# Start of a convolution and attention kernel: zero matmuls during the first load, first loads in two parts, `norms` two chunks later, the last v copied by two engines, the exp table set in the v phase

## The chip, the cores and the metric

The kernel runs on one core of a Trainium2 chip. It was written in Bass with the Tile framework. A core has a matmul engine (TensorE, PE in the profile), three engines for elementwise work (VectorE = DVE, ScalarE = ACT, GpSimd = POOL), SyncE (SP), which here only issues DMAs, a working memory (SBUF) and the matmul's result memory (PSUM, eight banks of 128 x 512 f32). ACT, SP and POOL each issue DMAs from a queue of their own, in program order, and an instruction behind a DMA in the program of ACT can only begin when that DMA could be issued.

The metric is the time of one execution on the device in microseconds. The profile is of one more execution, which took a little longer; all durations below are from it.

## The reference

Two layers on an input x of (2, 256, 64, 64). The first computes an attention over all 4096 positions with 8 heads of 32 channels, a 1x1 convolution of x and the result together, and a blend by an upsampled mask. The second has a channel gate, an attention in windows of 8 x 8, and two grouped 7 x 7 convolutions. The part that the change touches is the projection at the head of the first layer:

```python
def proj(Wp, bp):
    p = _conv1x1(x, Wp, bp)
    return p.reshape(B * NUM_HEADS, hd, num).transpose(0, 2, 1)
q = proj(Wq, bq) / math.sqrt(hd)
k = proj(Wk, bk)
v = proj(Wv, bv)
attn = jax.nn.softmax(jnp.einsum('bnd,bmd->bnm', q, k), axis=-1)
fuse = jnp.einsum('bnm,bmd->bnd', attn, v)
```

## The kernel before

Everything is f32. The order of the instructions on each engine is that of the program text (`tc.manual_schedule()`), and waits are derived from who writes and reads which tile. The work has four stages.

**q and k (lines 382 to 465, 0 to about 124 us).** x is cut into 16 chunks (2 images, 8 chunks of 512 positions, `chunks`). For each chunk PE computes q and k: for each, four matmuls of 128x128 weights by 128x512 (`L438`, output halves g by input halves kc), into a pair of PSUM banks from a pool of three such pairs. ACT copies the pair out with the bias (`qst`, `kst`, `L448`), squares it (`sq`, `L451`), and DVE takes maxima of the squares over groups of 16 (`top16`, `L457`). SP stores q and k to DRAM (`q_s`, `k_s`) and loads the x of a later chunk (`load_chunk`, `L406`), four chunks ahead. ACT's own queue also loads the weights: `WqT`, `WkT`, `WvT`, `bq`, `bk` before the loop (`L385`, `L394`), and four more small or large ones after each of the first chunks (`pending`, `L464`), from `WfT` to `ca_w2`. `prepared` is a generator that interleaves other preparation (masks, batch norms, convolution weights) with the chunks; it has a Sqrt on ACT near chunk 5 (`L285`).

Every DMA of the ACT and SP queues signals on one of eight semaphores, dealt out in turn; a DMA waits until the one that held its semaphore before has landed.

**norms (lines 411 to 418).** After every four chunks PE sums the `top16` maxima of those four over the channels of a head (four small matmuls, x8 in the profile) and DVE takes their maximum. In the text of before they come behind q and k of chunks 4, 8 and 12, and, for the last four chunks, behind v of chunk 0. The end of it is a flag (`L496` to `L501`, behind v of chunk 1) which says whether the exps need a shift; all engines read it at `L1299` and branch. In the run measured here no shift is needed.

**v (lines 470 to 516, about 124 to 180 us).** For each chunk eight matmuls with x as weights (`L475`), one ACT copy of 128x1024 out of the PSUM pair (`vst`, `L483`), two stores by POOL. Behind v of chunk 2 there is a small product for the bias (`bvf`, `L508`).

**Attention and the rest (from 180 us).** `psum.close()` gives PSUM to another layout; the first scores reuse banks that the v copies free. There are 1024 slots: scores of one key block for four heads (`sa`, `L643`, sixteen matmul records), exp on ACT (`ea`, `L656`, three instructions), the product with v (`ava`, `L695`), and a running sum of the exps on DVE (`L701`). Scores run two slots ahead of products. The sums of the first 64 slots are folded by POOL's DMAs into `folda` and summed over heads by PE (`dna`, `L729`). ACT's table of functions is set to exp by a one-element activation just ahead of the loop (`warm`, `L1235`). Between the slots PE also gets the matmuls of the second layer, and the convolutions end the kernel.

```python
if i and i % 4 == 0:
    norms(i // 4 - 1, last)
last = tops
```

Of the kernel before, what the change touches and what calls it, by code (L numbers as in the profile page):

```python
# [10 lines left out]
F32 = mybir.dt.float32  # L11
I32 = mybir.dt.int32
AF = mybir.ActivationFunctionType
# [6 lines left out]
P = 128  # L20
KC = C // P
CH = 512
# [12 lines left out]
WS = 8  # L35
NW = W // WS
# [21 lines left out]
def conv_seq_kernel(ctx: ExitStack, tc: tile.TileContext, a, out):  # L58
    nc = tc.nc
# [13 lines left out]
    def psum2(name):  # L73
        return ps["pair"].tile([P, 2, CH], F32, tag="s", name=name)

    def psum1(name):
        return ps["one"].tile([P, CH], F32, tag="h", name=name)
# [6 lines left out]
    ones = const.tile([P, P], F32, name="ones")  # L84
# [15 lines left out]
    for h in range(HEADS0):  # L100
        n, rows = (0, 32) if h < HG else (1 + (h - HG) // 2, 64)
        p = rows * (h % HG if h < HG else h % 2)
# [270 lines left out]
    warm = const.tile([1, 1], F32, name="warm")  # L373
    with (
        tc.tile_pool(name="mk", bufs=2) as mk,
        tc.tile_pool(name="w0", bufs=1) as w0,
        tc.tile_pool(name="st0", bufs=2) as st0,
        tc.tile_pool(name="x0", bufs=1) as x0,
        tc.tile_pool(name="cw", bufs=1) as cwp,
        tc.manual_schedule(),  # L380
    ):
        wqk = []
        for n in ("WqT", "WkT", "WvT"):
            t = w0.tile([P, KC, C], F32, name=n)
            nc.scalar.dma_start(t, a[n].rearrange("(k p) o -> p k o", p=P))  # L385
            wqk.append(t)
        wq, wk, wv = wqk
        bias = {}
        for n in ("bq", "bk"):

            t = w0.tile([P, KC], F32, name=n)
            src = a[n].rearrange("h d (g k) -> k (h d) g", g=KC)
            for k in range(2):
                nc.scalar.dma_start(t[64 * k : 64 * k + 64, :], src[k])  # L394
            bias[n] = t

        chunks = [(b, c) for b in range(B) for c in range(NCHUNK)]
        xs0 = []

        def load_chunk():  # L400
            if len(xs0) == len(chunks):
                return
            b, c = chunks[len(xs0)]
            x = x0.tile([P, KC, CH], F32, name=f"x0_{b}_{c}")
            src = a["x"][b].rearrange("(k p) h w -> p k (h w)", p=P)
            nc.sync.dma_start(x, src[:, :, c * CH : (c + 1) * CH])  # L406
            xs0.append(x)

        def norms(i, tops):
            s = psum1(f"nrm_{i}")
            for n in range(2 * KC):
                s_ = s[32 * n : 32 * n + 32, 0 : CH // 4]
                nc.tensor.matmul(
                    s_, headsum, tops[:, n].rearrange("p c n -> p (c n)"), start=True, stop=True
                )
            nc.vector.tensor_reduce(nm[:, i : i + 1], s[:, 0 : CH // 4], AX.X, ALU.max)

        prepared = prepare(mk, cwp)  # L420
        next(prepared)
        for _ in range(3):
            load_chunk()
        last = None
        for i, (b, c) in enumerate(chunks):
            load_chunk()
            x = xs0[i]
            sq = st0.tile([P, 2 * KC, CH], F32, tag="sq", name=f"sq_{b}_{c}")
            if i % 4 == 0:
                tops = st0.tile([P, 2 * KC, 4, CH // 16], F32, tag="top16", name=f"top16_{i}")  # L430
            for n, w in (("q", wq), ("k", wk)):
                s = psum2(f"{n}0_{b}_{c}")
                for g in range(KC):
                    for kc in range(KC):
                        rhs = x[:, kc, :]
                        if n == "q":
                            rhs = rhs.rearrange("p (r w c) -> p w r c", r=WS, w=NW)
                        nc.tensor.matmul(  # L438
                            s[:, g, :],
                            w[:, kc, g * P : (g + 1) * P],  # L440
                            rhs,
                            start=(kc == 0),
                            stop=(kc == KC - 1),
                        )
                t = st0.tile([P, KC, CH], F32, tag=n, name=f"{n}st_{b}_{c}")
                bt = bias["b" + n]
                for g in range(KC):
                    nc.scalar.activation(  # L448
                        t[:, g, :], s[:, g, :], AF.Identity, bias=bt[:, g : g + 1]
                    )  # L450
                nc.scalar.activation(sq[:, 0:KC] if n == "q" else sq[:, KC:], t, AF.Square)  # L451
                if n == "q":
                    nc.sync.dma_start(q_s[b, c], t.rearrange("p g n -> p (g n)"))
                else:
                    for g in range(KC):
                        nc.sync.dma_start(k_s[b, g, c], t[:, g, :])
            nc.vector.tensor_reduce(  # L457
                tops[:, :, i % 4], sq.rearrange("p g (n f) -> p g n f", f=16), AX.X, ALU.max
            )
            if i and i % 4 == 0:  # L460
                norms(i // 4 - 1, last)
            last = tops
            for t, src in pending[4 * i : 4 * i + 4]:
                nc.scalar.dma_start(t, src)  # L464
            next(prepared, None)


        row = psum1("toprow")
        top = w0.tile([P, 1], F32, name="top")
        for i, (b, c) in enumerate(chunks):  # L470
            s = psum2(f"v0_{b}_{c}")
            sv = s.rearrange("p a (t o) -> p (a t) o", t=2)
            for m in range(4):
                for kc in range(KC):
                    nc.tensor.matmul(  # L475
                        sv[:, m, :],
                        xs0[i][:, kc, m * P : (m + 1) * P],
                        wv[:, kc, :],
                        start=(kc == 0),
                        stop=(kc == KC - 1),  # L480
                    )
            v = st0.tile([P, KC, 4, P], F32, tag="v", name=f"vst_{b}_{c}")
            nc.scalar.copy(  # L483
                v.rearrange("p g m d -> p m g d"),
                sv.rearrange("p m (g d) -> p m g d", g=KC),
            )
            for g in range(KC):
                nc.gpsimd.dma_start(v_s[b, g, c], v[:, g].rearrange("p m d -> p (m d)"))
            if i == 0:
                norms(len(chunks) // 4 - 1, last)  # L490
                nc.vector.tensor_reduce(top, nm, AX.X, ALU.max)
            elif i == 1:

                nc.tensor.matmul(row[0:1, 0:P], top, ident, start=True, stop=True)
                qk2 = w0.tile([1, 2], F32, name="qk2")
                nc.vector.tensor_reduce(  # L496
                    qk2, row[0:1, 0:P].rearrange("p (i r) -> p i r", i=2), AX.X, ALU.max
                )
                prod = w0.tile([1, 1], F32, name="prod")
                nc.vector.tensor_mul(prod, qk2[:, 0:1], qk2[:, 1:2])  # L500
                nc.vector.tensor_scalar(flag, prod, (SAFE / SCALE0) ** 2, None, ALU.is_le)  # L501
            elif i == 2:


                s = psum1("bvf")
                for oc in range(KC):
                    for kc in range(KC):
                        nc.tensor.matmul(  # L508
                            s[:, oc : oc + 1],
                            wf[:, KC + kc, oc * P : (oc + 1) * P],  # L510
                            bv[:, kc : kc + 1],
                            start=(kc == 0),
                            stop=(kc == KC - 1),
                        )
                nc.vector.tensor_add(bf, s[:, 0:KC], bf)
            next(prepared, None)
        for _ in prepared:
            pass

    psum.close()  # L520

# [11 lines left out]
    def pipeline(arm, shifted, pools):  # L533
# [40 lines left out]
        def load_q(b, c):  # L574
            q = qp.tile([P, KC, CH], F32, tag="q", name=f"q{arm}_{b}_{c}")
            nc.sync.dma_start(q, q_s[b, c].rearrange("p (g n) -> p g n", g=KC))
            qts[b, c] = q
# [654 lines left out]

        banded = bands()

        nc.scalar.activation(warm, ones[0:1, 0:1], AF.Exp)  # L1235
        load_q(0, 0)
        for n in range(AHEAD):
            load_piece(n)
# [130 lines left out]
```

## Time and profile before

| what | us |
|---|---|
| three runs, median | 2900.6 (2898.96 to 2902.66) |
| the profiled execution | 2911.19, span 2909.3 |
| PE busy in the span | 2863.8 |
| first matmul | 5.47 |
| end of the last v matmul, about | 179.6 |
| first exp of the attention | 182.11 |

How to read it: the span is the time from the first to the last instruction of the profiled execution, and the execution's own time is 1.9 us more. Times in the chain of waits and in the timelines count from the span's start. A matmul of f32 shows as two records, so the eight records of q in a chunk are four instructions. `x8` behind an operation is the number of records that were merged, and their common length stands ahead. In brackets the idle time of the engine ahead of the group, with what ended it. `ACTq` and `SPq` are the queues' own work, the issuing of DMAs.

### The profile page before, as it was taken

To read this page: it belongs to the slowest core of one execution; us is meant where nothing else is said; L and a number is where in the kernel's file an instruction comes from. 1 tells how busy PE (TensorE), PEld (TensorE's weight loads), DVE (VectorE), ACT (ScalarE), POOL (GpSimd) and SP (SyncE) were. 2 spreads that over 40 slices of the span, in tenths; PEclk is the share of its full clock that TensorE was granted. 3 is DMA by queue.
4 is the path that set the end of the run, shared out by engine and by line. 5 is a ranking of instruction groups with operands and counts; after the bars stand their busy time and mean duration, and the time that the engine had idled before them with its cause. 6 is when DMAs were issued, how large, how long until landed. Compare 5 with 4: busy or idle time off the path is not lost.

```text
span 2909.3 us, 85471 instructions
## 1 busy us (share of the span) xinstructions
PE 2863.8 (98%) x37002; PEld 827.4 (28%) x37002; DVE 2435.4 (84%) x1344; ACT 2455.3 (84%) x4145; POOL 569.1 (20%) x937
## 2 busy tenths in 40 slices
PE   8999999999999999999999999999999999999998
PEld 3551122222222222222222222222222222222675
DVE  4249999899999999998999999999999899999211
ACT  5569989898989898989989898989899898989433
POOL 8111111111111212121111011111212110000476
PEclk9999999999999999999999999999999999999999
DMA  8545433433253434353333324343435342232565
GB/s 253 209 163 189 146 89 76 94 82 89 65 101 79 105 77 105 79 95 86 82 92 79 88 68 98 78 97 78 100 82 97 82 88 78 67 113 88 137 197 134
DMA packets 245690, 305.65 MB, mean 105 GB/s; under 512 B 121208, under 2 KB 137772, under 8 KB 245048
## 3 DMA queue, kind: packets, MB, share of 16 engines
q1 hardware_dynamic: 200068, 231.51, 28.6%
q0 software_dynamic: 40464, 65.79, 12.2%
q8 instruction: 293, 4.80, 0.7%
q10 hardware_dynamic: 4772, 2.79, 0.3%
q14 instruction: 93, 0.76, 0.1%
HBM read 221.88 MB, written 66.39 MB: 99 GB/s over the span
## 4 chain that ended last, share of the span: by engine, by line
PE 89%; DMA 4%; POOL 2%; issue 2%; DVE 2%; ACT 1%; ACTq 0%; POOLq 0%; DVEq 0%
PE sa L643 34%; PE ava L695 33%; PE qka L529 4%; PE hya L529 3%; PE c1a L1093 2%; PE vwa L529 2%; PE opa L529 2%; PE c2a L1118 2%; PE v L475 2%; PE q L438 2%; PE k L438 1%; DMA xs<-xo 1%; POOL out_dram L1172 1%; DMA invs<-inva 1%; DMA folda<-suma 1%
## 5 line engine op out<-in xcount | busy, mean ns | idle before, releaser
L656 ACT ACTIVATE ea<-sa 128x512 f32<-128x512 f32 (+1 forms) x3072 | 2037.0, 746 | 51.5 <-PE sa L643 24.5
L643 PE MATMUL sa<-qa,ka 32*64 32x512 f32 x16384 | 1147.5, 613 | 1.5 <-ACT vst L483 1.2
L701 DVE TENSOR_TENSOR suma<-suma,ea 128x2048 f32<-128x2048 f32 x480 | 1096.4, 2284 | 5.7 <-ACT ea L656 0.5
L695 PE MATMUL ava<-ea,va 128*32 128x512 f32 x8192 | 1091.8, 605 | 1.0
L701 DVE TENSOR_TENSOR odda<-odda,ea 128x2048 f32<-128x2048 f32 x420 | 958.4, 2282 | 45.9 <-ACT ea L656 45.8
L673 POOL DMA_DIRECT2D folda<-suma x336 | 235.7, 903 | 1669.6 <-DVE suma L703 981.6
L643 PEld LDWEIGHTS sa<-qa,ka 32*64 32x64 f32 x16384 | 242.4, 129 | 786.2 <-ACT ea L656 716.3
L695 PEld LDWEIGHTS ava<-ea,va 128*32 128x32 f32 x8192 | 161.6, 108 | 834.9 <-issue 805.4
L1172 POOL DMA_DIRECT2D out_dram<-za x212 | 119.7, 573 | 58.7 <-DVE za L1145 31.8
L701 DVE TENSOR_TENSOR suma<-ea,ea 128x2048 f32<-128x2048 f32 x32 | 73.2, 2286 | 58.9 <-ACT ea L656 58.9
L529 PE MATMUL qka<-ua,qkv_w 128*32 128x512 f32 x1024 | 115.8, 592 | 0.1
L785 ACT ACTIVATE ta<-hya,bf 128x512 f32<-128x512 f32 x32 | 20.3, 684 | 100.6 <-PE hya L529 94.6
L1024 POOL DMA_DIRECT2D xs<-xo x94 | 72.3, 1058 | 139.6 <-DVE xo L1009 137.4
L457 DVE TENSOR_REDUCE top<-sq 128x128 f32<-128x2048 f32 x16 | 36.6, 2285 | 74.8 <-ACT sq L451 74.8
L741 POOL DMA_DIRECT2D invs<-inva x62 | 34.2, 560 | 296.9 <-DVE inva L756 296.0
L1118 PE MATMUL c2a<-yca,wa 32*64 32x192 f32 (+1 forms) x2912 | 84.4, 367 | 3.7 <-issue 3.4
L903 ACT ACTIVATE ewa<-ewa,mxwa 128x64 f32<-128x64 f32 x256 | 85.3, 346 | 1.5 <-DVE mxwa L894 1.5
L1129 ACT ACTIVATE za<-c2a 128x384 f32<-128x384 f32 x64 | 27.8, 487 | 66.0 <-PE c2a L1118 38.5
L789 DVE TENSOR_TENSOR ta<-ta,mca 128x512 f32<-128x512 f32 x32 | 22.0, 688 | 67.1 <-ACT ta L785 67.1
L861 ACT ACTIVATE qka<-qka,qkv_b 128x512 f32<-128x512 f32 x64 | 40.2, 680 | 39.5 <-PE qka L529 39.5
L1118 PEld LDWEIGHTS c2a<-yca,wa 32*64 32x64 f32 x2912 | 67.5, 191 | 21.1 <-issue 13.9
L1145 DVE TENSOR_TENSOR za<-za,xla 128x768 f32<-128x768 f32 x16 | 15.3, 959 | 65.2 <-DMA out_dram<-za 36.4
(143 smaller groups left out, 1721.3 us busy)
## 6 DMA issues: line engine op xcount, KB each, us to landing
ka<-ks SPq DMA_DIRECT2D x256, 256.0 KB
va<-vs SPq DMA_DIRECT2D x256, 256.0 KB
wa<-ws SPq DMA_DIRECT2D x17, 896.0 KB
ws<-zeros SPq DMA_DIRECT2D x16, 896.0 KB
folda<-suma POOLq DMA_DIRECT2D x224, 64.0 KB, 3.2
folda<-suma POOLq DMA_DIRECT2D x112, 128.0 KB, 3.8
xs<-xo POOLq DMA_DIRECT2D x78, 140.0 KB, 8.1
x<-in_x_dram SPq DMA_DIRECT2D x16, 512.0 KB
```

Source lines behind the costliest of these rows:

```text
L438: nc.tensor.matmul(s[:, g, :], w[:, kc, g * P : (g + 1) * P], rhs, start=(kc == 0), stop=(kc == KC - 1),)
L475: nc.tensor.matmul(sv[:, m, :], xs0[i][:, kc, m * P : (m + 1) * P], wv[:, kc, :], start=(kc == 0), stop=(kc == KC - 1),)
L529: nc.tensor.matmul(out[o : o + 32], weights[:, o : o + 32], x, start=start, stop=stop)
L643: nc.tensor.matmul(heads[j][o], k[r, cols][:, o], q[r, g, :], start=True, stop=not shifted)
L656: nc.scalar.activation(e[:, h, :], tile, AF.Exp, scale=SCALE0)
L673: nc.gpsimd.dma_start(dst[p : p + rows], total[rows * k : rows * k + rows, h, :], accum_op=ALU.add if k else ALU.bypass,)
L695: nc.tensor.matmul(av[r, :], v[:, m % PB, r], e[:, j, :], start=start, stop=stop)
L701: nc.vector.tensor_add(total, first.pop(m % chains, total), e)
L903: nc.scalar.activation(e[:, n, :], e[:, n, :], AF.Exp, bias=mx[:, n : n + 1], accum_out=rs[:, n : n + 1],)
L1024: eng.dma_start(x_s[b, n, p + r0 : p + r1].rearrange("r g w -> g r w"), xo[64 * h : 64 * h + 64, oc, r0 - WS * c : r1 - WS * c, :],)
L1118: nc.tensor.matmul(tiles[j // 2][o, j % 2, 0 : n * W], w[r, d, o], y[r, 0:n, d : d + W], start=(d == 0), stop=(d == KS - 1),)
L1172: eng.dma_start(*args)
```

## The change

It has five parts, all in the first two stages.

- Two matmuls of zeros, 128x128 by 128x512, stand first on PE. DVE sets the zeros.
- `WqT` and x of chunk 0 are loaded by two DMAs each, one for each input half kc, instead of one. For chunk 0 the four matmuls of q, and of k, run with kc outside and the output half g inside.
- `norms` of chunks 0 to 3 stands behind q and k of chunk 6 instead of 4, the next ones behind 10 and 14, and the last behind v of chunk 1 instead of 0. `last` keeps the maxima of the last complete four. The flag is computed behind v of chunk 4 instead of 1, `bvf` behind 6 instead of 2.
- The last v is copied in halves, one by ACT and one by DVE.
- The one-element exp stands behind v of chunk 12 (with what is left of `prepared`, which had come to its end during the q and k stage), and no longer ahead of the attention.

```diff
+        idle = w0.tile([P, CH], F32, name="idle")
+        nc.vector.memset(idle, 0.0)
+        s = psum1("idle")
+        for n in range(2):
+            nc.tensor.matmul(s, idle[:, 0:P], idle, start=(n == 0), stop=(n == 1))
         wqk = []
         for n in ("WqT", "WkT", "WvT"):
             t = w0.tile([P, KC, C], F32, name=n)
-            nc.scalar.dma_start(t, a[n].rearrange("(k p) o -> p k o", p=P))
+            src = a[n].rearrange("(k p) o -> p k o", p=P)
+            for kc in range(KC if n == "WqT" else 1):
+                ks = slice(kc, kc + 1) if n == "WqT" else slice(0, KC)
+                nc.scalar.dma_start(t[:, ks], src[:, ks])
...
-            nc.sync.dma_start(x, src[:, :, c * CH : (c + 1) * CH])
+            for kc in range(1 if xs0 else KC):
+                ks = slice(0, KC) if xs0 else slice(kc, kc + 1)
+                nc.sync.dma_start(x[:, ks], src[:, ks, c * CH : (c + 1) * CH])
...
-                for g in range(KC):
-                    for kc in range(KC):
...
+                order = [(g, kc) for g in range(KC) for kc in range(KC)]
+                if i == 0:
+                    order.sort(key=lambda gk: gk[1])
+                for g, kc in order:
...
-            if i and i % 4 == 0:
+            if i > 4 and i % 4 == 2:
                 norms(i // 4 - 1, last)
-            last = tops
+            if i % 4 == 3:
+                last = tops
...
-            nc.scalar.copy(
-                v.rearrange("p g m d -> p m g d"),
-                sv.rearrange("p m (g d) -> p m g d", g=KC),
-            )
+            evict = [(nc.scalar.copy, slice(0, 4))]
+            if i == len(chunks) - 1:
+                evict = [(nc.scalar.copy, slice(0, 2)), (nc.vector.tensor_copy, slice(2, 4))]
+            for copy, ms in evict:
+                copy(
+                    v[:, :, ms].rearrange("p g m d -> p m g d"),
+                    sv[:, ms].rearrange("p m (g d) -> p m g d", g=KC),
+                )
...
-            if i == 0:
+            if i == 1:
                 norms(len(chunks) // 4 - 1, last)
...
-            elif i == 1:
+            elif i == 4:
...
-            elif i == 2:
+            elif i == 6:
...
-        for _ in prepared:
-            pass
+            if i == len(chunks) - 4:
+                for _ in prepared:
+                    pass
+                nc.scalar.activation(warm, ones[0:1, 0:1], AF.Exp)
...
-        nc.scalar.activation(warm, ones[0:1, 0:1], AF.Exp)
         load_q(0, 0)
```

More of the change, by code (lines that the diff above doesn't have):

```diff
@@ L432, in conv_seq_kernel @@
                 s = psum2(f"{n}0_{b}_{c}")
-                for g in range(KC):
-                    for kc in range(KC):
[L435 to L443, printed above, removed]
-                        )
+                order = [(g, kc) for g in range(KC) for kc in range(KC)]
+                if i == 0:
+                    order.sort(key=lambda gk: gk[1])
+                for g, kc in order:
+                    rhs = x[:, kc, :]
+                    if n == "q":
+                        rhs = rhs.rearrange("p (r w c) -> p w r c", r=WS, w=NW)
+                    nc.tensor.matmul(
+                        s[:, g, :],
+                        w[:, kc, g * P : (g + 1) * P],
+                        rhs,
+                        start=(kc == 0),
+                        stop=(kc == KC - 1),
+                    )
                 t = st0.tile([P, KC, CH], F32, tag=n, name=f"{n}st_{b}_{c}")
@@ L482, in conv_seq_kernel @@
             v = st0.tile([P, KC, 4, P], F32, tag="v", name=f"vst_{b}_{c}")
-            nc.scalar.copy(
-                v.rearrange("p g m d -> p m g d"),
-                sv.rearrange("p m (g d) -> p m g d", g=KC),
-            )
+            evict = [(nc.scalar.copy, slice(0, 4))]
[5 more added lines that the diff above has]
+                    sv[:, ms].rearrange("p m (g d) -> p m g d", g=KC),
+                )
             for g in range(KC):
                 nc.gpsimd.dma_start(v_s[b, g, c], v[:, g].rearrange("p m d -> p (m d)"))
-            if i == 0:
+            if i == 1:
                 norms(len(chunks) // 4 - 1, last)
                 nc.vector.tensor_reduce(top, nm, AX.X, ALU.max)
-            elif i == 1:
+            elif i == 4:
                 nc.tensor.matmul(row[0:1, 0:P], top, ident, start=True, stop=True)
```

## The prediction

> **What bounds the kernel now.** I read the page's busy shares first, then a table of busy time by stage, and then only the two ends of the stage that the change edits: the chain of waits, and the timelines of ScalarE (ACT) and TensorE (PE).
>
> ```profile
> PE 2863.8 (98%) x37002; PEld 827.4 (28%) x37002; DVE 2435.4 (84%) x1344; ACT 2455.3 (84%) x4145; POOL 569.1 (20%) x937
> ...
> 0.00:43.65 43.65, 36.38 (x80) 15.79 (x81) 10.44 (x14) 21.95 (x29) 33.54 (x83) 1.00 0.88 247
> ...
> 340.00:2700.00 2360.00, 2354.41 (x30040) 568.01 (x30032) 2191.65 (x1148) 2127.52 (x3627) 345.33 (x524) 1.00 0.38 87
> ```
>
> The table's rows give the stretch, its length, then the busy time of PE, PE's weight loads, DVE, ACT and POOL, the clock and the DMA share. From 340 to 2700 us PE is busy 2354.4 of 2360 us. So what the start saves is kept: the loop behind it has one bound, PE, and is shifted as a whole. At the start PE is busy 36.4 of 43.65 us: all that the change can win lies in holes of 7.3 us there (and in slow passes, below), 1.4 us before 125.77, and 1.5 us from 179.6 to 188.
>
> ```profile
> 18.23 10.72 DMA qkv_b<-in_qkv_b_dram
> ...
> 28.97 7.03 DMA out_w<-in_out_w_dram
> ...
> 41.22 2.30 DVE top L457
> 43.52 0.14 issue
> 43.65 0.43 PE nrm L415 x8
> ```
>
> The chain says that PE is not what sets the end of the first 43 us. PE runs q and k of chunk 0 (5.47 to 14.40), and then the chain leaves it: ACT stands in its own queue behind weight DMAs (10.72 us until `qkv_b` had landed, 7.03 us until `out_w` had), its squares come late, DVE's maximum comes later still, and PE stops 1.80 us for it in `norms`. ACT was out of that queue when `qst` of chunk 3 began, at 36.59. From the timelines:
>
> ```profile
> 10.40 1.28 ACT L448 ACT_TABLE_LOAD   x1 [10.40 <-DMA bk<-in_bk_dram]
> ...
> 125.77 0.42 PE L415 MATMUL nrm<-top,headsum 128*32 128x128 f32 x8 [1.40 <-DVE top L457]
> ...
> 180.71 1.28 ACT L1235 ACT_TABLE_LOAD   x1
> ...
> 180.79 3.02 PE L643 MATMUL sa<-qa,ka 32*64 32x512 f32 x32 [1.19 <-ACT vst L483]
> ...
> 182.11 18.44 ACT L656 ACTIVATE ea<-sa 128x512 f32<-128x512 f32 x28
> ```
>
> Each line has start, length, engine, line and operation, and in brackets the idle time before and what ended it. The first is where ACT begins; the second is the next hole (1.40 us, the fourth `norms`); the others are the third: PE waits 1.19 us for the last v copy (179.68, 1.01 us), and the exps start at 182.11, behind the table load.
>
> **What the Trainium skill says.** "TensorE: Matmul & The Clock Gate", Part 1: the array starts at half clock and is let go after a busy window of about 3.4 us, which runs free of the kernel. The trace agrees: weight loads of q start at 6.49, 7.34, 8.20 and 9.05 and then at 9.50 and 9.93, so a pass took 0.85 us until 3.6 us after the first matmul, and 0.43 from there. "ScalarE: Activation LUTs", What ACT_TABLE_LOAD costs: 1.28 us plus a drain of 1.38; the trace has the 1.28, and no drain (copy over at 180.69, load at 180.71). Table sets, same page: copies sit in every set, so the three v copies behind an early exp set cause no new load; before, the v copies followed Sqrt without one. "DMA: Bandwidth & Descriptors", Queues, rings and completion order: the SP and ACT queues take turns on the same 16 engines. The trace agrees: `WqT` (256 KB) and the first x (512 KB) were both there at 5.47.
>
> **The change, part by part**
>
> *Zero matmuls, first loads halved, kc outside in chunk 0.* The memset (128x512) is alone on DVE, which is idle until 16.81; POOL's 128x1120 memset took 1.04 us, so 0.2 to 0.6, I take 0.5. Two f32 matmuls are four passes (4 instructions of q show as x8), 4 x 0.85 = 3.4 us: from about 1.3 to 4.8 us. The first halves should land about half way between the first bytes (some 2 us) and 5.43, at about 4, and the second ones at 5.43 as now. q of chunk 0 then runs from 4.8 to 8.2 if the clock is let go at once, to 9.9 if the window's phase is worst, instead of to 10.95. So PE itself is 1.05 to 2.7 us early. But ACT starts at 10.40 when the bias `bq` lands, behind the same bytes in the same two queues (one more issue on ACT, 0.5 us, and one on SP, which puts the x of chunks 1 to 3 back by as much; the second `bq` now waits for the first half of `WqT`, about 4, where it was issued from about 3.5; both lie before the landing of what is ahead of it). So ACT begins as before. It gains only where it waited for PE: 0.37 us at `kst` of chunk 0. Everything behind in its queue, and SP's stores and x loads which follow ACT's results, moves by about that. The lanes on which one DMA waits for another keep the same pairs. x of chunk 2 now waits for the first half of x0; it has until about 19 us. The two queue waits end when `WfT` and `out_w` have landed, and these were issued 0.37 earlier. So `qst` of chunk 3 starts at 36.2 instead of 36.59, PE's k of chunk 4 (it needs that buffer) at about 37.9 instead of 38.25. In between PE, being early, waits for ACT: the lead goes into two stalls at k of chunks 2 to 4. Worth: 0.4 us; bounds 0 and 2.5 (if the ACT queue moved with PE).
>
> *norms two chunks later.* At chunk 4 PE goes straight to q of chunk 5: 1.80 us of waiting are gone. The eight matmuls (0.36 to 0.43) are done two chunks later, where the maximum has been ready for two chunks: no saving there, no cost. ACT is past its queue and needs some 4.5 us a chunk against PE's 6.9, so nothing else is late next; x of chunk 5 has landed by 33.75, when SP's next load on its lane went out. 1.80 us; bounds 1.5 and 1.9. In the v phase the fourth one, now behind v of chunk 1, comes 3.45 us later than at 124.37; it needed 125.77. 1.40 us, bounds 1.3 and 1.6. Row maximum, flag and `bf` move to chunks 1, 4 and 6: the flag is ready at about 138 instead of 131, and SP's first loads of q, k and v behind it have until 180.
>
> *Last v by two engines, exp set early.* ACT's half: a 512-wide ACTIVATE is 0.68 and a 1024-wide one 1.06, so the copy 0.63 for 1.01. DVE's half has no row; its adds run at 2.20 us for 2048, so 512 take 0.55 and some 0.12 to start: 0.67, bounds 0.6 and 0.8. PE is let go 0.34 us earlier. The table load moves into an ACT gap of 2.44 us (1.28 + 0.20 fit). Before, the first scores started at 180.79 and a slot takes 1.04, so exps could have begun at 181.9 and did at 182.11: 0.21. Together 0.55 us; bounds 0.2 and 0.9. What is late next is the exps' own pace: the first product needs slot 0's exps and then the scores of slot 2, 3.4 us behind the first exp as it was; that distance stays. DVE's sums start after the third slot's exps, and move with them.
>
> Sum: 0.4 + 1.8 + 1.4 + 0.55 = 4.15 us. The profiled execution took 2911.19 (span 2909.3) and would take 2907.0; the same 4.15 off the median of 2900.6 gives **2896.4 us**, 0.14% less. A measurement of this kernel can tell about 0.2% (5.8 us) from no change, so the likeliest outcome is a real gain just inside that bound.
>
> **Rivals**
>
> *More than 5.8 us (37%).* Two ways. If ACT's DMA waits slide with PE, the start gives 2.5 instead of 0.4: 6.25 us. And the first denominators end in a stretch at half clock:
>
> ```profile
> 339.78 0.43 PE L729 MATMUL dna<-folda,foldsum 128*32 128x128 f32 x8 [1.95 <-DMA folda<-suma]
> ...
> 340.13 2.01 PE L643 MATMUL sa<-qa,ka 32*64 32x512 f32 x16
> ```
>
> Scores take 1.04 us and products 1.00 in the loop; here 2.01, and then 1.79 for the products at 342.07: 1.7 more, because PE had waited for most of the window before. A shift of 4 us can put the wait across a window's edge: 4.15 + 1.7 = 5.9. Either alone is about 2894.5; both, 8 us, 2892.6. For it: the holes are there. Against: ACT's start hangs on `bq`, which the change doesn't move.
>
> *Swallowed (6%).* The stall at `norms` turns into a PSUM wait on ACT: 0 + 0 + 1.4 + 0.55, 2898.6. For it: ACT is behind in chunks 2 to 4. Against: k of chunk 3 was copied out at 40.1, before 41.3.
>
> *Slower (6%).* One mechanism: `bq` lands late. x and the weights now go out as more and smaller DMAs, and the second `bq` is issued later; if x of chunks 2 and 3 passes it, ACT starts late, and all up to chunk 4 follows one for one. 1 MB at some 390 GB/s (402 and 372 in the two slices of 2 us from 4 to 8) is 2.7 us, a gain of 1.5 left. From 4.15 us of delay on the kernel is slower than before, from 10 us on beyond the bound (2906.4). For it: DMA is full (share 0.98 to 1.07 from 4 to 10 us). Against: `bq` stands in ACT's queue in the same order.
>
> **How the numbers follow.** My own case has 51%, with its own range 2894.9 to 2898; the larger gain 37%, swallowed 6%, slower 6%. Own case and swallowed lie within 0.2%: 57%. The unknown costs reach from 0 + 1.5 + 1.3 + 0.2 = 3.0 to 2.5 + 1.9 + 1.6 + 0.9 = 6.9, with the clock 8.6; I leave out the slower case and the far ends of the others: 2892.0 to 2899.5.
>
> **What would show it.** Right: q of chunk 0 at 0.43 us a pass from near its start and over before 10; ACT's first table load still near 10.4; no wait of `norms` on DVE at either place; no table load between the last v copy and the first exp, which comes about 1.9 us after the last v matmul (2.5 before). Wrong: ACT's first load well off 10.4, `qst` of chunk 3 far from 36.2, a PE wait at q of chunk 5, or a different wait at the first denominators.

## The result, and the profile after

| | before | after |
|---|---|---|
| median of twelve runs | 2901.39 us (2897.03 to 2907.82) | 2897.16 us (2891.29 to 2903.18) |
| ratio, 95% interval | | 0.9984 [0.9976, 0.9992] |
| the profiled execution, its span | 2911.19, 2909.3 us | 2900.35, 2898.4 us |
| q of chunk 5 begins | 44.01 us | 42.12 us |
| last v matmul ends, about | 179.60 us | 176.68 us |
| first product (`ava`) begins | 185.59 us | 183.22 us |

The kernel is 0.16% faster, 4.2 us between the medians; the interval is 2.3 to 7.0 us (0.0008 and 0.0024 of 2901). The end of the last v matmul is the start of the first scores less the wait ahead of them, which the timelines print.

The page's busy times, of after:

```profile
PE 2866.6 (99%) x37006; PEld 828.1 (29%) x37006; DVE 2435.8 (84%) x1346; ACT 2455.4 (85%) x4145; POOL 570.3 (20%) x937
```

The table by stage, of after, with the columns as before (stretch, length, busy time of PE, its weight loads, DVE, ACT and POOL, clock, DMA share, GB/s):

```profile
0.00:43.65 43.65, 41.13 (x88) 17.68 (x89) 10.25 (x13) 21.18 (x28) 33.96 (x83) 1.00 0.87 245
340.00:2700.00 2360.00, 2356.26 (x30161) 571.80 (x30163) 2190.42 (x1148) 2128.28 (x3628) 347.98 (x528) 1.00 0.37 87
```

In the first 43.65 us PE is busy 41.1 us, where it was 36.4; about 3.8 of the 4.7 more are the zeros. The bound is the same: PE in the long loop, idle 3.7 of 2360 us there. Of the chain of waits of after, the DMAs in its first 38 us (start, length, what):

```profile
1.20 4.51 DMA WqT<-in_WqT_dram
...
6.31 4.42 DMA bk<-in_bk_dram
...
18.03 11.34 DMA qkv_b<-in_qkv_b_dram
...
31.18 6.04 DMA qs<-qst
```

They make up 26.3 of the chain's first 37 us, and ACT still waits for them; what has left the chain there is the pair of lines at 41 to 43 us, DVE's maximum and `norms`. From the timelines of after (start, length, engine, line and operation, idle time before and what ended it):

```profile
10.74 1.28 ACT L460 ACT_TABLE_LOAD   x1 [10.74 <-DMA bk<-in_bk_dram]
...
29.89 1.26 ACT L460 ACTIVATE qst<-q,bq 128x512 f32<-128x512 f32 x2 [5.97 <-DMA out_b<-in_out_b_dram]
...
31.21 3.70 PE L450 MATMUL k<-x,WkT 128*128 128x512 f32 x8 [0.82 <-ACT qst L460]
...
38.58 3.70 PE L450 MATMUL k<-x,WkT 128*128 128x512 f32 x8 [0.23 <-ACT qst L460]
42.12 3.60 PE L450 MATMUL q<-x,WqT 128*128 128x512 f32 x8
...
126.31 0.43 PE L425 MATMUL nrm<-top,headsum 128*32 128x128 f32 x8
...
176.76 0.59 ACT L500 COPY vst<-v 128x512 f32<-128x512 f32 x1 [2.44 <-PE v L488]
...
177.38 0.69 DVE L500 COPY vst<-v 128x512 f32<-128x512 f32 x1 [31.69 <-ACT vst L500]
...
178.43 2.97 PE L662 MATMUL sa<-qa,ka 32*64 32x512 f32 x32 [1.75 <-DVE vst L500]
...
179.67 11.26 ACT L675 ACTIVATE ea<-sa 128x512 f32<-128x512 f32 x17 [2.33 <-PE sa L662]
```

The reader is to see three things. Both waits of `norms` are gone: q of chunk 5 and the fourth `nrm` carry no bracket. PE, early now, waits twice for a `qst` copy, at k of chunks 3 and 4. And the split of the last v did not do what it says: DVE's half begins at 177.38, when ACT's half ends (176.76 + 0.59 = 177.35), and what ended its idle time is that half. PE waits 1.75 us for the pair, where it waited 1.19 for one copy by ACT.

Of the gain, 2.37 us are there at the first product (185.59 less 183.22). The two spans differ by 10.9 us. The other 8.5 us lie in the loop and the convolutions, which the change doesn't touch, and single executions of one kernel differ by as much (2891 to 2903 above). They are not read as an effect.

### The profile page after: what moved, and what is told of

Read it like the earlier page. It is cut to its first block, busy times and chain, and to the rows that moved or that the text cites. A ratio compares the mean times of both kernels' runs of the same rounds, so it can differ in the third digit from the quotient of the medians.

```text
span 2898.4 us, 85484 instructions
## 1 busy us (share of the span) xinstructions
PE 2866.6 (99%) x37006; PEld 828.1 (29%) x37006; DVE 2435.8 (84%) x1346; ACT 2455.4 (85%) x4145; POOL 570.3 (20%) x937
## 4 chain that ended last, share of the span: by engine, by line
PE 90%; DMA 4%; POOL 2%; issue 1%; DVE 1%; ACT 1%; ACTq 0%; SPq 0%; POOLq 0%; DVEq 0%
PE sa L662 35%; PE ava L714 33%; PE qka L548 4%; PE hya L548 3%; PE v L488 2%; PE opa L548 2%; PE vwa L548 2%; PE c1a L1112 2%; PE c2a L1137 2%; PE k L450 1%; PE q L450 1%; POOL out_dram L1191 1%; PE sca L901 1%; DMA folda<-suma 1%; DMA rda<-invs 1%
## 5 line engine op out<-in xcount | busy, mean ns | idle before, releaser
L722 DVE TENSOR_TENSOR suma<-suma,odda 128x2048 f32<-128x2048 f32 x30 | 68.8, 2292 | 1.0
```

Source lines behind the costliest of these rows:

```text
L722: nc.vector.tensor_add(acc[1], acc[1], acc[2])
```

## The experiments

Each ratio is to the kernel before, measured on the same chip. The runs below were made on three chips, and the kernel before itself took 2903 us on two of them and 2912 us on the third: ratios are compared, not times.

### Norms alone

The kernel before with the new places of `norms`, flag and `bf`; start, last v and exp table as before.

```diff
-            if i and i % 4 == 0:
+            if i > 4 and i % 4 == 2:
                 norms(i // 4 - 1, last)
-            last = tops
+            if i % 4 == 3:
+                last = tops
...
```

> The kernel before with the norms (and the flag and the bias product) moved as in the change, and nothing else of it. Theory (the whole gain lies here): ACT starts at 10.4 as before, q of chunk 5 follows k of chunk 4 at about 41.7 instead of 44.0, v begins about 1.9 us early, v ends about 3.4 us early (176.2 against 179.6), and the first product of the attention stands near 182.2, where it was 185.59 before and is 183.22 with the full change. So the total is about 3.4 us under before, at least as fast as the full change. Rival (the three other parts bring their share, as the prediction had it): the first product later than 183.2.

Measured: 0.9990 [0.9981, 0.9998]. The timeline of PE, this kernel:

```profile
11.55 3.60 PE L438 MATMUL k<-x,WkT 128*128 128x512 f32 x8
...
42.45 3.60 PE L438 MATMUL q<-x,WqT 128*128 128x512 f32 x8
...
178.21 3.02 PE L644 MATMUL sa<-qa,ka 32*64 32x512 f32 x32 [1.19 <-ACT vst L484]
```

From k of chunk 0 to q of chunk 5 it is 30.90 us: nine steps of 3.43, PE back to back. In the kernel before it was 33.22 (10.79 to 44.01), with 1.80 of waiting and 0.36 for the matmuls of `norms` in it. The first scores come 2.58 us earlier than before (178.21 against 180.79), although this execution's k of chunk 0 was 0.76 later. So the moved `norms` are worth 2.58 + 0.76 = 3.34 us in this pair of profiles, and nothing that was hidden came up in their place. The first product stood at 183.01, later than the theory's 182.2 by about the 0.76 us of the late start and earlier than the rival's 183.2; the ratio's 2.9 us (0.6 to 5.5) agrees with 3.34.

### Last v by ScalarE alone

The changed kernel, with the last copy as it was before and the exp table early.

```diff
-            if i == len(chunks) - 1:
-                evict = [(nc.scalar.copy, slice(0, 2)), (nc.vector.tensor_copy, slice(2, 4))]
...
```

> The full change with the last v copied by ACT alone, in one piece, as before. Theory (the two halves ran one after the other, 0.59 and then 0.69 us, since DVE's half waits for ACT's): PE waits 1.2 us for the last v instead of 1.75, the first exp comes about 2.3 to 2.4 us after the last v matmul instead of 2.99, the first product near 182.6 instead of 183.22. Rival (the halves help): the first product at 183.5 or later.

Measured: 0.9979 [0.9971, 0.9986]. From the timelines:

```profile
174.69 1.01 ACT L496 COPY vst<-v 128x1024 f32<-128x1024 f32 x1 [2.44 <-PE v L488]
...
175.80 2.97 PE L658 MATMUL sa<-qa,ka 32*64 32x512 f32 x32 [1.19 <-ACT vst L496]
...
177.04 13.30 ACT L671 ACTIVATE ea<-sa 128x512 f32<-128x512 f32 x20 [1.34 <-PE sa L658]
...
180.59 1.07 PE L710 MATMUL ava<-ea,va 128*32 128x512 f32 x8
```

PE's wait is 1.19 again. From the end of the last v matmul (175.80 less 1.19) to the first product it is 5.98 us; in the changed kernel 183.22 less 176.68 is 6.54, in the kernel before 5.99. So the split costs 0.56 us. The first product stood at 180.59 and not near 182.6, since PE was already 2.08 us earlier at q of chunk 5 (40.04 against 42.12), for a reason that the section after next gives. This run also isolates the early table: the first exp comes 1.24 us after the first scores start, 1.32 before, and the first product 4.79 us after, 4.80 before. The early exp table is worth nothing that can be read here.

### No zero matmuls, and whole first loads

Two kernels, each the changed one without one part of its start.

```diff
...
-        for n in range(2):
-            nc.tensor.matmul(s, idle[:, 0:P], idle, start=(n == 0), stop=(n == 1))
```

> The full change without the zero matmuls. Theory (the early clock is lost in ACT's start): q of chunk 0 starts near 4.8 and ends later than 9.78, at about 10.2, ACT's first table load stays near 10.7, and q of chunk 5 and the first product stay within 0.2 us of 42.12 and 183.22. Rival (PE's lead is worth something): q of chunk 5 at 42.6 or later.

```diff
-            for kc in range(KC if n == "WqT" else 1):
-                ks = slice(kc, kc + 1) if n == "WqT" else slice(0, KC)
-                nc.scalar.dma_start(t[:, ks], src[:, ks])
+            nc.scalar.dma_start(t, a[n].rearrange("(k p) o -> p k o", p=P))
...
-                if i == 0:
-                    order.sort(key=lambda gk: gk[1])
```

> The full change with WqT and the first x loaded by one DMA each, and chunk 0 in the old order. Theory (the halved loads put the bias back by 0.3 us, and ACT with it): ACT's first table load near 10.4 instead of 10.74, q of chunk 3's copy at about 36.7 instead of 37.26, q of chunk 5 near 41.6 instead of 42.12. Rival (the halves let PE begin early, and that counts): q of chunk 5 at 42.3 or later.

(The second also loads the x of chunk 0 whole.) Measured: 0.9990 [0.9983, 0.9997] without the zeros and 0.9993 [0.9985, 1.0002] with whole loads. The timeline of PE, first of the kernel without zeros, then of the one with whole loads:

```profile
4.66 5.90 PE L445 MATMUL q<-x,WqT 128*128 128x512 f32 x8 [4.66 <-DMA WqT<-in_WqT_dram]
10.39 3.60 PE L445 MATMUL k<-x,WkT 128*128 128x512 f32 x8
...
41.30 3.60 PE L445 MATMUL q<-x,WqT 128*128 128x512 f32 x8
```

```profile
5.51 4.59 PE L443 MATMUL q<-x,WqT 128*128 128x512 f32 x8 [0.27 <-DMA WqT<-in_WqT_dram]
9.94 3.60 PE L443 MATMUL k<-x,WkT 128*128 128x512 f32 x8
...
40.84 3.60 PE L443 MATMUL q<-x,WqT 128*128 128x512 f32 x8
```

The times expected for q of chunk 5 missed in both runs, the rivals' too: it begins earlier than in the changed kernel's own profile (42.12), although a part of the start was taken away. In neither does PE wait for ACT between chunk 0 and chunk 5 (30.9 us both). Whether the two waits on `qst` belong to the changed kernel is tried in the next section; here the time to look at is k of chunk 0. It stands at 9.94 with whole loads and at 10.39 without zeros, against 8.34 to 9.73 for the full start (next section).

### The changed kernel once more, and without its start

> The changed kernel itself, profiled once more. Theory (what stood in its first profile at k of chunks 3 and 4, 1.6 us in all between k of chunk 0 and q of chunk 5, came from the moment at which a transfer landed behind ScalarE's queue, which varies): q of chunk 5 begins 30.9 to 31.2 us after k of chunk 0, as in the other profiles with this start, and no wait on a q store is over 0.3 us. Rival (it belongs to the program): the same two waits, 32.5 us. In either case VectorE's half copy of the last v begins after ScalarE's and TensorE waits 1.75 us.

In the kernel without its start there are no zeros, the first loads are whole and chunk 0 has the old order; everything else is the change's.

> The changed kernel without its start: no zero matmuls, whole first loads, the old order of kc and g in chunk 0; norms, last v and exp table as in the change. Theory (the start is worth about 2 us wherever TensorE then runs back to back to chunk 5, and not the 0.4 of the prediction): k of chunk 0 begins at 10.7 to 11.6 us, q of chunk 5 30.9 us after it (41.6 to 42.5), the first product at 182.4 to 183.5, and the time is 1.5 to 3 us above the changed kernel's 2897.2 (ratio to the kernel before 0.9989 to 0.9995). Rival (the prediction's 0.4 was right and the rest lay elsewhere): the ratio stays at 0.9984 to 0.9987.

Measured without the start: 0.9988 [0.9980, 0.9995]; k of chunk 0 at 11.64, q of chunk 5 at 42.54, the first product at 183.64, each 0.04 to 0.14 us later than the theory's range. The ratio lies between what the two theories expected and decides nothing; the profile is read instead. The changed kernel's second profile is of one execution; its time, 2911.98 us, stands beside 2907 to 2919 us for the kernel before on the same chip, and nothing is read from it. Its timeline of PE, and two pieces of its chain of waits:

```profile
4.90 3.60 PE L450 MATMUL q<-x,WqT 128*128 128x512 f32 x8
8.34 3.60 PE L450 MATMUL k<-x,WkT 128*128 128x512 f32 x8
...
30.05 3.70 PE L450 MATMUL k<-x,WkT 128*128 128x512 f32 x8 [0.95 <-ACT qst L460]
...
40.45 3.60 PE L450 MATMUL q<-x,WqT 128*128 128x512 f32 x8
```

```profile
15.13 10.17 DMA WfT<-in_WfT_dram
...
25.32 3.39 DMA out_b<-in_out_b_dram
```

Neither expectation held for the waits on `qst`: one wait of 0.95 us at k of chunk 3, and none at chunk 4. (PE's wait for the last v was 1.75 us again, as expected.) Together with the two other kernels whose first 45 us are the same program, the wait follows from two times that both vary. PE is due at k of chunk 3 20.60 us after k of chunk 0, and the PSUM pair that it needs is free when `qst` of chunk 2 ends:

| profile | k of chunk 0 | k of chunk 3 due | `qst` of chunk 2 ends | lost up to chunk 5 | q of chunk 5 |
|---|---|---|---|---|---|
| after | 9.62 | 30.22 | 31.15 | 1.60 | 42.12 |
| after, again | 8.34 | 28.94 | 30.00 | 1.21 | 40.45 |
| last v by ACT alone | 9.04 | 29.64 | 29.59 | 0.10 | 40.04 |
| two banks (below) | 9.73 | 30.33 | 29.53 | 0.00 | 40.63 |

"Lost" is the distance from k of chunk 0 to q of chunk 5 less the 30.90 of a PE that never waits. Where `qst` is later than PE is due, the lead is lost; where not, it is kept, but for 0.10 us where the two meet.

What the start is worth hangs on what it is compared with, since k of chunk 0 varies without it too: it began at 10.79 in the kernel before, at 11.55 with norms alone and at 11.64 in this run, and up to there the three are the same program. A PE that never waits has q of chunk 5 at 41.69, 42.45 and 42.54 then; the first is an estimate, 10.79 + 30.90, because the kernel before waits in `norms` on the way. The mean is 42.23, and 40.81 with the start. So the start is worth 1.4 us on average, and anything from -0.4 (41.69 against 42.12) to 2.5 (42.54 against 40.04) in a pair of profiles. The ratios with and without it, 0.9984 and 0.9988, do not tell the two apart.

Why k of chunk 0 varies is seen in the weight loads of PE, first of after, then of its second profile:

```profile
1.46 0.50 PEld L386 LDWEIGHTS idle<-idle 128*128 128x128 f32 x2 [1.46 <-DVE idle L383]
...
4.77 0.60 PEld L450 LDWEIGHTS q<-x,WqT 128*128 128x128 f32 x2 [1.11 <-DMA WqT<-in_WqT_dram]
5.89 0.34 PEld L450 LDWEIGHTS q<-x,WqT 128*128 128x128 f32 x1 [0.52 <-issue]
6.74 0.34 PEld L450 LDWEIGHTS q<-x,WqT 128*128 128x128 f32 x1 [0.52 <-issue]
7.48 0.19 PEld L450 LDWEIGHTS q<-x,WqT 128*128 128x128 f32 x1 [0.40 <-issue]
7.91 0.19 PEld L450 LDWEIGHTS q<-x,WqT 128*128 128x128 f32 x1 [0.24 <-issue]
```

```profile
1.46 0.50 PEld L386 LDWEIGHTS idle<-idle 128*128 128x128 f32 x2 [1.46 <-DVE idle L383]
...
4.50 0.59 PEld L450 LDWEIGHTS q<-x,WqT 128*128 128x128 f32 x2 [0.83 <-DMA WqT<-in_WqT_dram]
5.33 0.19 PEld L450 LDWEIGHTS q<-x,WqT 128*128 128x128 f32 x1 [0.24 <-issue]
5.76 0.19 PEld L450 LDWEIGHTS q<-x,WqT 128*128 128x128 f32 x1 [0.24 <-issue]
```

The zeros begin at 1.46 in both. Full pace, 0.43 us from load to load, is there from 7.48 in one and from 5.33 in the other. Without zeros it moves as well: the first matmul stands at 5.47 in the kernel before and in this run, full pace from 9.50 and from 11.21. "TensorE: Matmul & The Clock Gate", Part 1, of the Trainium skill says that the window which counts activity runs free of the kernel; these two executions of one program agree: the same zeros bought a full q of chunk 0 at speed (3.60 us) once and some of it (4.75 us) the other time.

### Out-weight loads two per chunk

```diff
-            for t, src in pending[4 * i : 4 * i + 4]:
+            for t, src in pending[2 * i : 2 * i + 2]:
```

> The changed kernel with two of the out-weight loads issued from ScalarE's queue per chunk in place of four (the same loads, over four chunks instead of two). Theory (where the first six chunks run late, it is ScalarE standing behind its own DMA issues that gates TensorE): no wait of TensorE on a ScalarE store of q in chunks 2 to 4 is longer than 0.3 us, q of chunk 5 begins at 39.5 to 40.5 us against 42.12 in the changed kernel's profile, the time falls by 1 to 2 us where the gate would have been shut. Rival (the transfers themselves fill the memory path): the third chunk's q store again at 36 us or later and q of chunk 5 at 41.5 us or later.

Measured: 0.9986 [0.9977, 0.9995]. The timelines of ACT and PE:

```profile
23.86 1.26 ACT L460 ACTIVATE qst<-q,bq 128x512 f32<-128x512 f32 x2 [2.47 <-DMA WfT<-in_WfT_dram]
...
8.54 3.60 PE L450 MATMUL k<-x,WkT 128*128 128x512 f32 x8
...
39.44 3.60 PE L450 MATMUL q<-x,WqT 128*128 128x512 f32 x8
```

`qst` of chunk 2 begins at 23.86 in place of 28.3 to 29.9 and ends 4.0 us before PE is due at k of chunk 3; PE is back to back (8.54 to 39.44 is 30.90). So the lead is lost to ACT standing in its own queue behind eight issues. The rival's times did not come, and from 15 to 30 us the DMA engines were as busy as in the changed kernel (a mean share of 0.95, for 0.94 and 0.95 in its two profiles). Why each landing that ACT waits for takes as long as it does is not shown by this. The expected gain on the changed kernel in time was not seen: the intervals of the two overlap almost wholly.

### Biases from SP's queue

```diff
-                nc.scalar.dma_start(t[64 * k : 64 * k + 64, :], src[k])
...
-        for _ in range(3):
+        load_chunk()
...
+                nc.sync.dma_start(t[64 * k : 64 * k + 64, :], src[k])
...
+        for _ in range(2):
             load_chunk()
```

> The changed kernel with the two bias vectors loaded from SP's queue, behind the x of chunk 0, in place of ScalarE's. Theory (ScalarE's first activation stands behind the bias issues in its own queue): its first table load moves from 10.74 to between 6 and 8 us and its first q store begins within 0.5 us of the end of the first q matmuls, with q of chunk 5 at 40 to 40.5 us if no other gate is met. Rival (the later DMA issues on ScalarE's queue gate it, not the first store): the first store early, q of chunk 5 at 41.5 us or later all the same.

Measured: 0.9982 [0.9974, 0.9989]. The timeline of ACT:

```profile
7.16 1.28 ACT L461 ACT_TABLE_LOAD   x1 [7.16 <-DMA bq<-in_bq_dram]
9.69 1.26 ACT L461 ACTIVATE qst<-q,bq 128x512 f32<-128x512 f32 x2 [1.24 <-PE q L451]
...
27.46 1.26 ACT L461 ACTIVATE qst<-q,bq 128x512 f32<-128x512 f32 x2 [5.07 <-DMA out_b<-in_out_b_dram]
```

ACT starts 3.1 to 3.6 us earlier than in the four profiles above, and its first `qst` follows PE by 0.04 us. But `qst` of chunk 2, behind eight out-weight issues, began at 27.46, 0.8 to 2.4 earlier than in the table above: the rest of the early start is spent waiting at those issues. The first activation is not what holds PE: q of chunk 5 stood at 40.63, inside the spread of the four profiles above. That is a little later than the theory had it and well before the rival's 41.5; PE lost 0.25 us between k of chunk 0 (9.48) and there.

### The last v in two PSUM banks

The last v tile goes into two tiles of one PSUM bank each, and the copies into two SBUF tiles, so that the two engines share nothing.

```diff
+            if final:
+                banks = [psum1(f"vl{n}").rearrange("p (t o) -> p t o", t=2) for n in range(2)]
...
+                for n, copy in enumerate((nc.scalar.copy, nc.vector.tensor_copy)):
+                    h = st0.tile([P, KC, 2, P], F32, tag=f"half{n}", name=f"vlast{n}", bufs=1)
```

> The last v tile is computed into two tiles of one PSUM bank each, copied out by ScalarE and VectorE into two separate SBUF tiles; everything else is the changed kernel's. Theory (the split failed because both copies read one PSUM tile and wrote one SBUF tile, so that VectorE's came after ScalarE's): VectorE's copy now starts within 0.3 us of ScalarE's, TensorE's last wait before sa is between 0.6 and 1.0 us in place of 1.75, and the first product begins 5.2 to 5.8 us after the last v matmul (6.52 in the changed kernel, 5.99 with ScalarE's copy alone), a gain of about 1 us on the changed kernel. Rival (what counts is the exp and DVE chain behind the first sa, not the copy): 5.9 us or more again.

Measured: 0.9982 [0.9975, 0.9990]. From the timelines of ACT, DVE and PE:

```profile
173.50 0.58 ACT L502 COPY vlast<-vl 128x512 f32<-128x512 f32 x1 [0.67 <-PE vl L492]
...
175.23 0.69 DVE L502 COPY vlast<-vl 128x512 f32<-128x512 f32 x1 [31.03 <-PE vl L492]
...
176.28 2.97 PE L675 MATMUL sa<-qa,ka 32*64 32x512 f32 x32 [1.09 <-DVE vlast L502]
```

DVE now waits for PE and not for ACT. But the two copies do not run at once. ACT begins when its bank is complete, at 173.50, and is over at 174.08; DVE begins when the last matmul is, 1.73 us behind ACT and not within 0.3 us as the theory had it. So that the shared tiles put the halves in order in the changed kernel is argued, from the bracket (DVE's half begins 0.03 us after ACT's ends, and is let go by it) and from the way waits are derived; whether the PSUM tile or the SBUF tile did it was not tried, and no run here has the two copies side by side.

PE's wait of 1.09 us and the first product, 5.88 us after the last v matmul (181.07 less 175.19), missed what the theory expected, too; the product is only 0.1 better than with ACT alone. What PE waits for is DVE's half, 0.69 us, and then 0.36 us more before the first scores begin (176.28 less 175.92). Behind ACT's copy that distance is 0.10 us (175.80 less 175.70 with ACT alone). It is not the same behind all that DVE does: in the kernel before, `nrm` began 0.14 us after DVE's maximum had ended (the `issue` piece at 43.52 of its chain). Why it is longer behind this copy is open.

### The three edits together, and the two engines exchanged

> The three edits together: two one-bank PSUM tiles for the last v, two out-weight loads per chunk, biases from SP's queue. If each does what its theory says: q of chunk 5 at 39.5 to 40.5 us, the first product at 179.0 to 180.5 us against 183.22, and the time 4 to 8 us below the kernel before (ratio 0.9972 to 0.9986), at or below the version with ScalarE's copy alone (0.9979). Rival (the start is worth nothing because a later stage takes it back): first product early by 2 to 3 us, the ratio 0.9984 or nearer to one.

Measured: 0.9965 [0.9952, 0.9979], 2893.22 us beside 2902.88. q of chunk 5 at 39.77 and the first product at 180.21, both as expected. The ratio is lower than expected, and the interval holds the lower half of what was expected. At the first product this kernel is 5.4 us ahead of the kernel before (185.59 less 180.21), where the ratio says 10 us (6.1 to 13.9). The ratio rests on five executions, and where the rest of it lies is not shown.

Then, with DVE on the first half and ACT on the second:

```diff
-                for n, copy in enumerate((nc.scalar.copy, nc.vector.tensor_copy)):
+                for n, copy in enumerate((nc.vector.tensor_copy, nc.scalar.copy)):
```

> The three edits together, with VectorE copying the first half of the last v and ScalarE the second. Theory (the wait before the first scores is the last half's copy and the signal after it: VectorE's 0.69 with 0.40 behind it, ScalarE's 0.58 with 0.18): the wait falls from 1.09 to 0.75 to 0.8 us and the first product begins 5.5 to 5.6 us after the last v matmul in place of 5.88; the time within 1 us of the version before the swap (ratio 0.9960 to 0.9972), since 0.3 us is below what the times resolve. Rival (the wait also holds something other than the copy): 1.0 us or more.

Measured: 0.9971 [0.9956, 0.9985]. From the timelines:

```profile
173.14 0.69 DVE L503 COPY vlast<-vl 128x512 f32<-128x512 f32 x1 [29.30 <-PE vl L493]
...
174.86 0.59 ACT L503 COPY vlast<-vl 128x512 f32<-128x512 f32 x1 [2.40 <-PE vl L493]
...
175.55 2.97 PE L676 MATMUL sa<-qa,ka 32*64 32x512 f32 x32 [0.72 <-ACT vlast L503]
```

PE's wait is 0.72 us, a little less than expected, and the first product begins 5.51 us after the last v matmul (180.34 less 174.83), as expected: 0.48 us better than the kernel before, 1.03 better than the change. Both versions lie below the changed kernel by their ratios, but the intervals still touch its own ([0.9976, 0.9992]); that they beat it is likely and not settled. They beat the kernel before.

## Why the prediction was right, and where it was wrong

The predicted time, 2896.4 us, is 0.8 us from the measured 2897.16, and 0.14% was predicted where 0.16% was measured. Two of its terms were wrong by about 1 us, in opposite directions, and cancelled. That the sum came out so close is luck; that it came out near 3 to 4 us is not, since 3.2 us of it are the moved `norms`, which were right.

- **Moved norms, 1.80 + 1.40 = 3.2 us: right.** Norms alone gave 3.34 us between two profiles. In the change, from the first v matmul to the end of the last it was 57.4 us and not 58.9. No wait took the place of the two removed.
- **Start, 0.4 us with bounds 0 and 2.5: the stall foreseen, its size taken as fixed.** The zeros ran from 1.46 to 5.24 (predicted 1.3 to 4.8), their memset took 0.48 (0.5), q of chunk 0 was over at 9.78 and 8.50 (8.2 to 9.9), and ACT's table load stayed near 10.4 (10.74, 10.29). `qst` of chunk 3, predicted at 36.2, came at 37.26 and 35.12. The mis-sized term is "the lead goes into two stalls at k of chunks 2 to 4". In the first profile that is what happened, at chunks 3 and 4, and against the profile of before it left nothing (q of chunk 5 at 42.12, where 10.79 + 30.90 is 41.69). But it rests on when one copy ends, and that moved between 29.5 and 31.2 us over the four profiles with the same first 45 us. In two of them PE lost 1.2 and 1.6 us there, in two 0.1 or nothing, and the start was worth 1.4 us on average. The prediction had read a landing time and a start of k from one profile as constants of the kernel.
- **Last v and exp table, 0.55 us: wrong, and the sign too.** The step that failed is "PE is let go 0.34 us earlier", which took the two halves to run side by side. The durations were right (0.59 and 0.69 for 0.63 and 0.67). But DVE's half came behind ACT's, and PE was let go 0.56 us later; both copies read one PSUM tile and write one SBUF tile, and the waits are derived from the tiles. Even where DVE's half waited for PE alone, it left a gain of 0.1 us, with the 0.36 us behind it. The exp that was to come 1.9 us after the last v matmul came at 2.99. The 0.21 us for the exp was wrong as well: the exp began 1.24 us after the first scores with the table long set, where the prediction took 1.1, and the first product did not follow it. That an early table costs nothing was right: the load (1.28 us at 167.43) lies in a gap of ACT, and the three copies and the exps behind it bring no other, which is what "ScalarE: Activation LUTs", Table sets, of the Trainium skill says of copies.
- **The sum** by the runs: 1.4 + 3.34 - 0.56 = 4.2 us, for 4.15 predicted and 4.2 [2.3, 7.0] measured. In the pair of profiles of before and after, with -0.43 for the start, the same sum is 2.35, and 2.37 is what the first product shows.
- **The rivals.** The larger gain's first way, "ACT's DMA waits slide with PE", is not what happened: ACT was let go earlier in three of four profiles (`qst` of chunk 2 at 28.3 to 28.7, for 29.85 in before), but earliest (28.27) where PE was latest (k of chunk 0 at 9.73). Its second did not happen either: the slow stretch behind the first denominators is still there in after (a product of 1.93 us at 338.39 and scores of 1.87 at 340.26). The late `bq` of the slower rival was 0.34 us in one profile and not late at all in the other.

What stays open: why `qst` of chunk 2 is let go at different times. The chain of waits names the loads: in after ACT's last issue ahead of it waits for `qkv_b`, which lands at 29.37, and in the second profile the chain runs through `WfT` (25.30) and `out_b` (28.71). Why they land when they do was not tried. Open too is which shared tile orders the two halves of the last v, and what makes up the 0.36 us behind DVE's copy.

## What to carry to other kernels

A copy split between two engines need not run in parallel. Look for the other engine's name in the bracket of the second half; here halves that shared a PSUM tile and an SBUF tile ran one after the other. Give the last half to the engine whose copy, and the distance from it to the waiting matmul, are shorter together (0.59 and 0.10 us by ACT, 0.69 and 0.36 by DVE). A stall that depends on where a transfer lands needs more than one profile before it is priced: take the mean of several, and bounds from their spread. A gain at the head of a long loop with one bound is read from landmarks in the profile (first product, first chunk) when it is smaller than the scatter of the time; in ten of the eleven kernels measured here the gain at the first product lies inside the interval of the ratio, all but the three edits together. The kernel before needs more than one profile as well: its k of chunk 0 stood 0.76 us later in the kernel with norms alone, which is the same program up to there.

## What was unexpected of the hardware

- Behind a copy by DVE the waiting matmul began 0.36 us after the copy's end, behind one by ACT 0.10 us (within 0.01 us in all profiles that show it: 178.07 to 178.43 and 175.92 to 176.28; 180.69 to 180.79 and 175.45 to 175.55). Behind DVE's maximum it was 0.14 us.
- 3.8 us of matmuls of zeros bought full speed at 5.3 us in one execution and at 7.5 in another of the same program, with the zeros at the same place.
- The same eight DMA issues held the third `qst` back until 29.9 us in one execution and 28.7 in another of one program, and until 28.3 in two kernels that are the same up to there.
